# A ConvNeXt block and a Mamba block on one core: batch groups of the convolution, weights on another queue, one transfer for each scan tile

## The chip, the cores and the metric

The kernel runs on one core of a Trainium2 chip. The metric is the device time of one execution in microseconds; the number given for a kernel is the median of its runs. PE is TensorE, DVE VectorE, ACT ScalarE, POOL GpSimd and SP SyncE, which issues nearly all DMAs here. All data is float32.

## The reference, cut to what matters

The input is 32 images of 96 channels and 56 x 56 points (3136 tokens).

```
# layer 0
h = depthwise_conv7x7(x) + conv_b
h = layernorm over channels(h)
x1 = (gelu(h @ w1 + b1) @ w2 + b2) * layer_scale + x
# layer 1: two Mamba layers on seq = x1 as (batch, 3136 tokens, 96)
xs, z = split(layernorm(seq) @ in_w)               # 192 channels each
xc = silu(causal conv of 4 taps over tokens(xs) + conv_b)
dt, Bm, Cm = split(xc @ xproj_w)                   # 6, 16 states, 16 states
delta = softplus(dt @ dt_w + dt_b)
dA  = exp(delta * A);   dBx = delta * Bm * xc      # per channel and state
h_t = dA_t * h_(t-1) + dBx_t                       # 192 x 16 recurrences
y = (sum over states(h * Cm) + Dp * xc) * silu(z)
seq = seq + y @ out_w
# then: 1x1 convolution over (seq, pooled x1), batch norm over everything, + x1
```

## The kernel before

**Tiles of the scan.** An image is cut into 4 chunks of 784 tokens (`CH`), each of two halves of 392 (`HC`). The 192 x 16 recurrences of a chunk are 24 scans of 128 partitions: 6 blocks `j` of 32 channels and 4 groups `g` of 4 states. A partition of a scan tile is one channel of the block with one of the group's four states; before the change the order is (state, channel), that is partition 32 s + m. One chunk in one Mamba layer is a *stage*; there are 256, numbered from 0, and each has 24 *steps*, one scan each.

**A step** (`scan`, `exps`, `spread`, `pooled`, `add_up`). ACT makes `exp(delta * A)` from the tile `d4` of the block (L871). The tile dBx comes in two ways. For blocks 2 and 5 (`POOLED`), POOL multiplies `us` (u = delta * xc, read back with copies for the four states) by the states' B (L897). For the others, PE spreads `u` into PSUM with the 0/1 matrix `sel` (L886, tile `w`) and DVE multiplies it by B (L913). DVE scans (L920) into a ring of four tiles `h`, POOL multiplies by C (L924), and PE sums the four states with `ssum` into `y` (L957). B and C are in `bc` tiles, one per group, with B in the first half of the row and C in the second. `bc`, `d4` and `us` are read from DRAM copies (`bd`, `dd`, `uu`) of small on-chip results, since a DMA can repeat a row for several partitions: `load_bc`, `load_d4` and `load_u` each issue four DMAs per tile, one for each state of the group.

**The order by hand.** The loop is emitted in a fixed order: every other piece of work has a slot, counted in steps of the stage, and `run` emits it there. `prep` prepares the next stage, `post` finishes the last one, `block0` does half a chunk of layer 0 for the following images (its `norm`, tile `hz`, L429, is on DVE at slot 14.1), and `conv` does one channel pair of the 7 x 7 convolution for one group of images. Each of `block0` and `conv` has its slots in one stage at a time, from stage 2 on.

**The convolution.** Two channels x 56 rows fill 112 partitions; the seven vertical taps are in a banded 112 x 112 matrix per horizontal tap. The first group of images goes ahead of the loop (`conv_pair`, 48 pairs, three rotating buffers): DVE fills the bands (L165), SP stores them to `band_d`, PE does 7 matmuls for each half of the images (L176), ACT evicts (`ct`, L180), SP stores. The other groups go through the loop, `NB` images each, two parts of 7 taps (L541), at slots 7.7 to 10.4 and 18.5 to 22.2, with the bands read back. With `NB = 7` there are 11 images ahead and 3 groups x 48 pairs = 144 stages with a convolution (2 to 145).

```
    NB = 7
    b0 = B - 3 * NB if B > 3 * NB else B
...
            at = (7.7, 8.2, 8.6, 9.2, 9.6, 10.2, 10.4), (18.5, 18.6, 19.2, 20.2, 21.2, 21.3, 22.2)
...
            if 2 <= m < len(convs) + 2:
                put(m, conv(*convs[m - 2]))
```

**Ahead of the loop.** After three pairs of the convolution come the weights (about 60 DMAs on SP, in `column`, `blocks`, `norm_weights` and beside them), then the other 45 pairs. There the order is the compiler's priorities, not written by hand, and each queue works in order. Then `block0` makes the first image's eight halves, with ACT alternating between Ln and Exp (the inverse root), Gelu and plain functions; functions of different sets make ACT load a table (`ACT_TABLE_LOAD`). Last, `prep` of stage 0 runs without anything beside it.

**After the loop** the batch norm is applied in a pass over all images.

Of the kernel before, what the change touches and what calls it, by code (L numbers as in the profile page):

```python
# [34 lines left out]
F32 = mybir.dt.float32  # L35
I32 = mybir.dt.int32
AF = mybir.ActivationFunctionType
ALU = mybir.AluOpType
# [6 lines left out]
C = 96  # L45
# [16 lines left out]
def convnext_mamba_kernel(  # L62
# [142 lines left out]
    for a in range(2):  # L205
        r = slice(64 * a, 64 * a + 64)
        for jj in range(2):
            nc.vector.tensor_copy(
                sel[r, jj, :].rearrange("p (s m) -> p s m", s=4),
                ident[r, 64 * a + 32 * jj : 64 * a + 32 * jj + 32]  # L210
                .unsqueeze(1)
                .broadcast_to([64, 4, 32]),
            )
# [3 lines left out]
    nc.vector.tensor_tensor(ssum, ssum, ident[:, 64:96], ALU.add)  # L217
    nc.vector.tensor_tensor(ssum, ssum, ident[:, 96:128], ALU.add)

    def column(src, n, name):  # L220
        t = const.tile([n, 1], F32, name=name, tag=name)
        nc.sync.dma_start(t, src)
        return t

    def blocks(src, name):

        n = src.shape[1]
        t = const.tile([128, NQ, n], F32, name=name, tag=name)
        for a in range(2):
            nc.sync.dma_start(t[64 * a : 64 * a + 64], src.rearrange("(q m) n -> m q n", m=64))  # L230
        return t

    g0, be0 = column(ln0_g, C, "g0"), column(ln0_b, C, "be0")
# [5 lines left out]
    nc.sync.dma_start(ls, lscale.rearrange("c one -> one c").partition_broadcast(128))  # L239
    for f in range(NF):  # L240
        nc.sync.dma_start(b1_sb[:, f : f + 1], b1[f * 128 : (f + 1) * 128, :])
        nc.sync.dma_start(w2_sb[:, f, :], w2[f * 128 : (f + 1) * 128, :])
        nc.vector.tensor_tensor(w2_sb[:, f, :], w2_sb[:, f, :], ls, ALU.mult)
    gpw_sb = const.tile([C, C], F32, name="gpw_sb")
    nc.sync.dma_start(gpw_sb, gp_wt)
    gpb = column(gp_b, C, "gpb")
    fw1 = const.tile([C, C], F32, name="fw1")
    nc.sync.dma_start(fw1, fus_wt[0:C, :])
    fw2 = const.tile([C, C], F32, name="fw2")
    nc.sync.dma_start(fw2, fus_wt[C : 2 * C, :])  # L250
    fusb = column(fus_b, C, "fusb")
    bng, bnb = column(bn_g, C, "bng"), column(bn_b, C, "bnb")

# [3 lines left out]
    def norm_weights(dst, src, g, b):  # L257


        n = src.shape[1]  # L260
        raw = su.tile([C, n], F32, name="raw", tag="raw")
        nc.sync.dma_start(raw, src)
        m = su.tile([C, C + 1], F32, name="m", tag="nm")
        nc.vector.tensor_scalar(m[:, 0:C], center_m, g, None, ALU.mult)
        nc.vector.tensor_copy(m[:, C : C + 1], b)
        ps = sups.tile([128, 512], F32, name="ps", tag="nps")
        nc.tensor.matmul(ps[0 : C + 1, 0:n], m, raw, start=True, stop=True)
        nc.vector.tensor_copy(dst, ps[0 : C + 1, 0:n])

    norm_weights(w1_sb, w1, g0, be0)  # L270
    for i in range(2):
        d = {}
        lg, lb = column(ln_g[i], C, f"lg{i}"), column(ln_b[i], C, f"lb{i}")
        wz = const.tile([C + 1, 2 * DIN], F32, name=f"inw{i}", tag=f"inw{i}")
        norm_weights(wz, in_w[i], lg, lb)
        wx = const.tile([C + 1, 4, DIN], F32, name=f"wx{i}", tag=f"wx{i}")
        nc.sync.dma_start(wx, taps[i].partition_broadcast(C + 1))
# [24 lines left out]
        nc.sync.dma_start(dtw, dt_w[i])  # L302
# [34 lines left out]
    with ExitStack() as main:  # L337
# [55 lines left out]
        def block0(b, c, s):  # L393
# [45 lines left out]
            def gelu():  # L439
                v["gl"] = work([128, NF, HC], "gl", 1)  # L440
                for f in range(NF):
                    nc.scalar.activation(
                        v["gl"][:, f], v["pss"][f][:, 0:HC], AF.Gelu, bias=b1_sb[:, f : f + 1]
                    )
                exp_ln_tables()

            def down():
                v["ps"] = psum(2)
# [48 lines left out]
        with tc.tile_pool(name="p0", bufs=1) as p0, tc.tile_pool(  # L497
            name="pp0", bufs=1, space=PSUM
        ) as pp0:
            pre += [p0, pp0]  # L500
            pieces = [
                (slot + 3 * (2 * c + s), piece)
                for c in range(NCH)
                for s in range(2)
                for slot, *_, piece in block0(0, c, s)
            ]
            for _, piece in sorted(pieces, key=lambda p: p[0]):
                piece()
            pre.clear()

        wp = main.enter_context(tc.tile_pool(name="wp", bufs=2))
# [64 lines left out]
        def prep(S):  # L576
# [142 lines left out]
            def load_u(k):  # L719
                def piece():  # L720
                    t = wp.tile([128, CH], F32, name="us", tag="us", bufs=1)
                    for s in range(4):
                        nc.sync.dma_start(t[32 * s : 32 * s + 32], v["uu"][k])
                    S.us[POOLED[k]] = t

                return piece

            def load_d4(j):
                def piece():
                    t = wp.tile([128, CH], F32, name="d4", tag="d4", bufs=3)  # L730
                    for s in range(4):
# [388 lines left out]
```

## Time and profile before

| | us |
|---|---|
| median of 3 runs (lowest, highest) | 17344.25 (17338.93, 17366.62) |
| the profiled execution, its own time | 17343.56 |
| its span in the profile | 17341.9 |
| last eviction of the first convolution | starts at 433.07 |
| first scan | 574.21 |
| start of stage 2 | 717.04 |
| last scan | 16978.6 |
| final pass | 16998 to 17342 |

The span is the profiled execution from its first to its last instruction. A group's row gives line, engine, operation, tiles and shapes, then the count after `x`, the busy time, the mean of one in ns, and the engine's idle time just before with what ended most of it. A row of the waits says which instruction's engine stood still for which, in total, how often and how long at most. A row of the timeline is start, duration, engine, line and operation, with the idle time before it in brackets; rows of several instructions give the whole stretch. PEclk is the share of PE's clock that was granted.

### The profile page before, as it was taken

The page shows a single profiled execution, that of the slowest core. Times are in us where ns is not written, and L with a number is a line of the kernel's source. Part 1 is how long each engine was busy: PE and PEld are TensorE (multiplying, and loading weights), DVE is VectorE, ACT ScalarE, POOL GpSimd, SP SyncE. Part 2 cuts the span into 40 slices and gives each one's busy share as a digit, 9 for nine tenths or more (in the row PEclk, how much of TensorE's full clock was granted, in tenths as well). Part 3 has the DMA queues.
Part 4 walks back from the last instruction along what each step waited for, and adds up shares of the span by engine and source line. Part 5 has one row for each costly group of instructions (what it writes and reads, how often), then busy time and mean ns, then how long its engine had stood idle before and what let it go on. Part 6 is the DMA issues. An engine that isn't in the chain of part 4 may idle for free. (4 is left out here: it accounts for less than half of the span.)

```text
span 17341.9 us, 217468 instructions
## 1 busy us (share of the span) xinstructions
PE 15452.2 (89%) x67992; PEld 5467.0 (32%) x67992; DVE 16061.7 (93%) x12345; ACT 11459.0 (66%) x18648; POOL 15637.1 (90%) x8737
## 2 busy tenths in 40 slices
PE   8899999999999999999999988888888888888870
PEld 5233333333333333333333322222222222222220
DVE  8699999999999999999999999999999999999994
ACT  1666666666676776666666666666666666666653
POOL 0699999999999999999999999999999999999991
PEclk9899999999999999999999999999999999999985
DMA  4455555555555555555555555555555555555548
GB/s 107 105 138 140 139 136 139 139 140 140 133 141 140 140 140 135 138 140 140 137 136 141 137 129 125 124 131 127 124 126 128 128 125 124 131 128 125 127 113 280
DMA packets 1421981, 2346.44 MB, mean 135 GB/s; under 512 B 629958, under 2 KB 793586, under 8 KB 1420820
## 3 DMA queue, kind: packets, MB, share of 16 engines
q1 hardware_dynamic: 1413652, 2294.00, 53.5%
q10 hardware_dynamic: 7168, 38.54, 0.6%
q8 instruction: 536, 8.78, 0.2%
q14 instruction: 625, 5.12, 0.1%
HBM read 1929.11 MB, written 402.41 MB: 134 GB/s over the span
## 5 line engine op out<-in xcount | busy, mean ns | idle before, releaser
L924 POOL TENSOR_TENSOR da<-h,bc 128x784 f32<-128x784 f32 x6144 | 11295.2, 1861 | 799.0 <-DVE h L920 686.1
L920 DVE TENSOR_TENSOR_SCAN h<-da,st,w 128x784 f32<-128x784 f32 x3072 | 5664.2, 1844 | 324.0 <-ACT st L931 9.4
L957 PE MATMUL y<-da,ssum 128*32 128x392 f32 x24576 | 5131.2, 540 | 429.9 <-POOL da L924 427.5
L913 DVE TENSOR_TENSOR w<-w,bc 128x784 f32<-128x784 f32 x4096 | 3995.7, 976 | 284.0 <-PE w L886 114.6
L897 POOL TENSOR_TENSOR da<-us,bc 128x784 f32<-128x784 f32 x2048 | 3816.3, 1863 | 2.9 <-DMA us<-uu 2.9
L871 ACT ACTIVATE da<-d,A 128x784 f32<-128x784 f32 x4096 | 3757.6, 941 | 43.6 <-DMA d<-dd 27.7
L871 ACT ACTIVATE w<-d,A 128x784 f32<-128x784 f32 x2048 | 1878.8, 918 | 2662.8 <-DVE h L920 2270.2
L920 DVE TENSOR_TENSOR_SCAN h<-w,st,da 128x784 f32<-128x784 f32 x1536 | 2712.4, 1827 | 5.9 <-ACT w L871 4.8
L622 PE MATMUL ps<-hn,wx 97*64 97x392 f32 x12288 | 2262.6, 503 | 7.9 <-DVE hn L610 7.9
L957 PEld LDWEIGHTS y<-da,ssum 128*32 128x32 f32 x24576 | 1093.7, 115 | 3700.0 <-issue 2095.1
L920 DVE TENSOR_TENSOR_SCAN h<-da,w 128x784 f32<-128x784 f32 x1024 | 1827.0, 1784 | 107.9 <-ACT st L931 3.8
L886 PE MATMUL w<-u,sel 64*128 64x392 f32 x4096 | 1028.4, 581 | 638.5 <-DVE h L920 637.4
L622 PEld LDWEIGHTS ps<-hn,wx 97*64 97x64 f32 x12288 | 795.3, 136 | 1429.1 <-issue 1111.3
L701 POOL TENSOR_TENSOR u<-dl,xc 128x784 f32<-128x784 f32 (+1 forms) x512 | 736.8, 1439 | 543.0 <-ACT dl L687 543.0
L951 PE MATMUL y<-xc,D 128*128 128x392 f32 x1536 | 796.6, 604 | 252.1 <-DVE z L938 246.1
L541 PE MATMUL ps<-xpad,band 112*112 112x224 f32 (+1 forms) x4032 | 1003.0, 358 | 0.0
L361 ACT ACT_TABLE_LOAD x759 | 973.8, 1283 | 14.5 <-PEq L1107 0.8
L370 ACT ACTIVATE sq<-ps 96x392 f32<-96x392 f32 x768 | 340.7, 490 | 812.6 <-PE ps L365 464.3
L920 DVE TENSOR_TENSOR_SCAN h<-w,da 128x784 f32<-128x784 f32 x512 | 872.3, 1766 | 0.0
L541 PEld LDWEIGHTS ps<-xpad,band 112*112 112x112 f32 x4032 | 583.8, 175 | 832.5 <-issue 783.5
L679 PE MATMUL ps<-dbl,dtw 6*64 6x392 f32 x3072 | 688.3, 511 | 99.9 <-ACT dbl L657 99.9
L886 PEld LDWEIGHTS w<-u,sel 64*128 64x128 f32 x4096 | 327.7, 196 | 1229.6 <-DVE h L920 1055.3
(124 smaller groups left out, 14412.7 us busy)
## 6 DMA issues: line engine op xcount, KB each, us to landing
bc<-bd SPq DMA_DIRECT2D x4096, 196.0 KB, 5.3
d<-dd SPq DMA_DIRECT2D x6144, 98.0 KB, 2.8
us<-uu SPq DMA_DIRECT2D x2048, 98.0 KB, 2.2
dd<-dl SPq DMA_DIRECT2D x512, 294.0 KB, 3.8
uu<-u SPq DMA_DIRECT2D x1024, 49.0 KB, 1.6
band<-band_d SPq DMA_DIRECT2D x144, 343.0 KB, 3.5
cv<-conv_d SPq DMA_DIRECT2D x256, 147.0 KB, 2.4
xin<-in_x SPq DMA_DIRECT2D x128, 294.0 KB, 3.8
```

The source lines that it names most:

```text
L361: nc.scalar.preload_act_table_set("natural_log_exp_and_others")
L541: nc.tensor.matmul(v["ps"][0:R2, 0 : (last - first) * W], v["band"][:, dw, :], xpad[:, first:last, dw : dw + W], start=(dw == 0), stop=(dw ...
L622: nc.tensor.matmul(v["x", q][rows(a), 0:HC], weights[:, k, 64 * q : 64 * q + 64], v["hn"][:, o : o + HC], start=(k == 0), stop=(k == last),)
L701: nc.gpsimd.tensor_tensor(S.u[:, lo:hi], v["dl"][:, lo:hi], S.xc[:, lo:hi], ALU.mult)
L871: nc.scalar.activation(e, S.d4[j], AF.Exp, scale=S.d["A"][:, j, g : g + 1])
L886: nc.tensor.matmul(S.u4[:, 512 * a : 512 * a + HC], sel[rows(a), j % 2, :], S.u[rows(a), j // 2, :], start=True, stop=True,)
L897: nc.gpsimd.tensor_tensor(t, S.us[j], S.bcs[g][:, 0, :], ALU.mult)
L913: nc.vector.tensor_tensor(halves(db), S.u4.rearrange("p (a b) -> p a b", a=2)[:, :, 0:HC], halves(S.bcs[g][:, 0, :]), ALU.mult,)
L920: nc.vector.tensor_tensor_scan(ring[:, g, :], S.e.pop((j, g)), db, 0.0 if c == 0 else d["st"][:, j, g : g + 1], ALU.mult, ALU.add,)
L924: nc.gpsimd.tensor_tensor(da, ring[:, g, :], S.bcs[g][:, 1, :], ALU.mult)
L951: nc.tensor.matmul(S.y[:, 0:HC], S.d["D"][:, q, :], S.xc[:, q, :], start=True, stop=False)
L957: nc.tensor.matmul(S.y[r0 : r0 + 32, 0:HC], ssum, da[:, tok(a)], start=False, stop=(g == NG - 1),)
```

## The change

1. `NB` becomes 5: 12 images ahead of the loop, 4 groups of 5 in it, so 192 stages (2 to 193) with a convolution of 3 + 2 images instead of 4 + 3.
2. A scan tile's partitions are ordered (channel, state), 4 m + s. So `load_d4` and `load_u` can bring a tile with one DMA that repeats each row four times, and `load_bc` a half of a `bc` tile with one DMA that repeats four rows 32 times: 16 instead of 48 DMAs in a stage. `sel`, `ssum` and `A` follow the new order; `A` is now gathered with a mask `own` instead of by partition blocks.
3. All weights ahead of the loop, but those of the first convolution, are issued from POOL: 61 DMAs in the place of 57 on SP.
4. In the first image, the two halves of a chunk have the same slots, instead of following one another, and the requests for the Ln and Exp table are placed before the pair's root.

```diff
-    NB = 7
-    b0 = B - 3 * NB if B > 3 * NB else B
+    NB = 5
+    b0 = B - 4 * NB if B > 4 * NB else B
...
-                sel[r, jj, :].rearrange("p (s m) -> p s m", s=4),
+                sel[r, jj, :].rearrange("p (m s) -> p m s", s=4),
...
-    nc.vector.tensor_tensor(ssum, ident[:, 0:32], ident[:, 32:64], ALU.add)
...
+    nc.vector.tensor_reduce(ssum, ident.rearrange("p (m s) -> p m s", s=4), AX.X, ALU.add)
+    own = su.tile([128, 4], F32, name="own", bufs=1)
+    nc.vector.tensor_reduce(own, ident.rearrange("p (m s) -> p s m", s=4), AX.X, ALU.add)
+    nc.vector.tensor_scalar(own, own, -1.0, None, ALU.mult)
...
-        nc.sync.dma_start(t, src)
+        nc.gpsimd.dma_start(t, src)
...
-        for s in range(4):
-            r = slice(32 * s, 32 * s + 32)
-            nc.sync.dma_start(ar[r], a_log[i].rearrange("(q m) n -> m q n", m=32))
-            nc.scalar.activation(A[r], ar[r, :, s::4], AF.Exp)
-        nc.vector.tensor_scalar(A, A, -1.0, None, ALU.mult)
+        for j in range(2 * NQ):
+            src = a_log[i][32 * j : 32 * j + 32, :]
+            nc.gpsimd.dma_start(ar[:, j, :], src.unsqueeze(1).broadcast_to([32, 4, NS]))
+        nc.scalar.activation(ar, ar, AF.Exp)
+        nc.vector.tensor_scalar(A, ar[:, :, 0::4], own[:, 0:1], None, ALU.mult)
+        for s in range(1, 4):
+            nc.vector.scalar_tensor_tensor(
+                A, ar[:, :, s::4], own[:, s : s + 1], A, ALU.mult, ALU.add
+            )
...
             def root():
+                if pre and s == 0:
+                    exp_ln_tables()
                 rsqrt(v["ps"])
...
-                exp_ln_tables()
+                if not pre:
+                    exp_ln_tables()
...
-                (slot + 3 * (2 * c + s), piece)
+                (slot + 4 * c, piece)
...
+            exp_ln_tables()
             pre.clear()
...
-                        for s in range(4):
+                        for k in range(2):
+                            src = v["bd"][NS * k + 4 * g : NS * k + 4 * g + 4, :]
                             nc.sync.dma_start(
-                                t[32 * s : 32 * s + 32],
-                                v["bd"][4 * g + s :: NS, :].partition_broadcast(32),
+                                t[:, k, :], src.unsqueeze(0).broadcast_to([32, 4, CH])
                             )
...
-                    for s in range(4):
-                        nc.sync.dma_start(t[32 * s : 32 * s + 32], v["uu"][k])
+                    nc.sync.dma_start(t, v["uu"][k].unsqueeze(1).broadcast_to([32, 4, CH]))
...
-                        nc.sync.dma_start(
-                            t[32 * s : 32 * s + 32], v["dd"][32 * j : 32 * j + 32, :]
-                        )
+                    src = v["dd"][32 * j : 32 * j + 32, :]
+                    nc.sync.dma_start(t, src.unsqueeze(1).broadcast_to([32, 4, CH]))
```

More of the change, by code (lines that the diff above doesn't have):

```diff
@@ L208, in convnext_mamba_kernel @@
             nc.vector.tensor_copy(
-                sel[r, jj, :].rearrange("p (s m) -> p s m", s=4),
+                sel[r, jj, :].rearrange("p (m s) -> p m s", s=4),
                 ident[r, 64 * a + 32 * jj : 64 * a + 32 * jj + 32]
-                .unsqueeze(1)
-                .broadcast_to([64, 4, 32]),
+                .unsqueeze(2)
+                .broadcast_to([64, 32, 4]),
             )
     ssum = const.tile([128, 32], F32, name="ssum")
-    nc.vector.tensor_tensor(ssum, ident[:, 0:32], ident[:, 32:64], ALU.add)
-    nc.vector.tensor_tensor(ssum, ssum, ident[:, 64:96], ALU.add)
-    nc.vector.tensor_tensor(ssum, ssum, ident[:, 96:128], ALU.add)
+    nc.vector.tensor_reduce(ssum, ident.rearrange("p (m s) -> p m s", s=4), AX.X, ALU.add)
+    own = su.tile([128, 4], F32, name="own", bufs=1)
+    nc.vector.tensor_reduce(own, ident.rearrange("p (m s) -> p s m", s=4), AX.X, ALU.add)
+    nc.vector.tensor_scalar(own, own, -1.0, None, ALU.mult)
     def column(src, n, name):
         t = const.tile([n, 1], F32, name=name, tag=name)
-        nc.sync.dma_start(t, src)
+        nc.gpsimd.dma_start(t, src)
         return t
@@ L229, in blocks @@
         for a in range(2):
-            nc.sync.dma_start(t[64 * a : 64 * a + 64], src.rearrange("(q m) n -> m q n", m=64))
+            nc.gpsimd.dma_start(t[64 * a : 64 * a + 64], src.rearrange("(q m) n -> m q n", m=64))
         return t
@@ L238, in convnext_mamba_kernel @@
     ls = su.tile([128, C], F32, name="ls", bufs=1)
-    nc.sync.dma_start(ls, lscale.rearrange("c one -> one c").partition_broadcast(128))
+    nc.gpsimd.dma_start(ls, lscale.rearrange("c one -> one c").partition_broadcast(128))
     for f in range(NF):
-        nc.sync.dma_start(b1_sb[:, f : f + 1], b1[f * 128 : (f + 1) * 128, :])
-        nc.sync.dma_start(w2_sb[:, f, :], w2[f * 128 : (f + 1) * 128, :])
+        nc.gpsimd.dma_start(b1_sb[:, f : f + 1], b1[f * 128 : (f + 1) * 128, :])
+        nc.gpsimd.dma_start(w2_sb[:, f, :], w2[f * 128 : (f + 1) * 128, :])
         nc.vector.tensor_tensor(w2_sb[:, f, :], w2_sb[:, f, :], ls, ALU.mult)
     gpw_sb = const.tile([C, C], F32, name="gpw_sb")
-    nc.sync.dma_start(gpw_sb, gp_wt)
+    nc.gpsimd.dma_start(gpw_sb, gp_wt)
     gpb = column(gp_b, C, "gpb")
     fw1 = const.tile([C, C], F32, name="fw1")
-    nc.sync.dma_start(fw1, fus_wt[0:C, :])
+    nc.gpsimd.dma_start(fw1, fus_wt[0:C, :])
     fw2 = const.tile([C, C], F32, name="fw2")
-    nc.sync.dma_start(fw2, fus_wt[C : 2 * C, :])
+    nc.gpsimd.dma_start(fw2, fus_wt[C : 2 * C, :])
     fusb = column(fus_b, C, "fusb")
@@ L261, in norm_weights @@
         raw = su.tile([C, n], F32, name="raw", tag="raw")
-        nc.sync.dma_start(raw, src)
+        nc.gpsimd.dma_start(raw, src)
         m = su.tile([C, C + 1], F32, name="m", tag="nm")
@@ L276, in convnext_mamba_kernel @@
         wx = const.tile([C + 1, 4, DIN], F32, name=f"wx{i}", tag=f"wx{i}")
-        nc.sync.dma_start(wx, taps[i].partition_broadcast(C + 1))
+        nc.gpsimd.dma_start(wx, taps[i].partition_broadcast(C + 1))
         for k in range(4):
@@ L301, in convnext_mamba_kernel @@
         dtw = const.tile([DTR, DIN], F32, name=f"dtw{i}", tag=f"dtw{i}")
-        nc.sync.dma_start(dtw, dt_w[i])
+        nc.gpsimd.dma_start(dtw, dt_w[i])
         d["dtw"] = dtw
@@ L730, in piece @@
                     t = wp.tile([128, CH], F32, name="d4", tag="d4", bufs=3)
-                    for s in range(4):
-                        nc.sync.dma_start(
-                            t[32 * s : 32 * s + 32], v["dd"][32 * j : 32 * j + 32, :]
-                        )
+                    src = v["dd"][32 * j : 32 * j + 32, :]
+                    nc.sync.dma_start(t, src.unsqueeze(1).broadcast_to([32, 4, CH]))
                     S.d4.append(t)
```

## The prediction

> **What bounds the kernel now.** I read the page's busy rows, then the timeline for the length of a stage, then VectorE's waits, then the windows for the clock.
>
> ```profile
> span 17341.9 us, 217468 instructions
> PE 15452.2 (89%) x67992; PEld 5467.0 (32%) x67992; DVE 16061.7 (93%) x12345; ACT 11459.0 (66%) x18648; POOL 15637.1 (90%) x8737
> ...
> L924 POOL TENSOR_TENSOR da<-h,bc 128x784 f32<-128x784 f32 x6144 | 11295.2, 1861 | 799.0 <-DVE h L920 686.1
> L920 DVE TENSOR_TENSOR_SCAN h<-da,st,w 128x784 f32<-128x784 f32 x3072 | 5664.2, 1844 | 324.0 <-ACT st L931 9.4
> ...
> L913 DVE TENSOR_TENSOR w<-w,bc 128x784 f32<-128x784 f32 x4096 | 3995.7, 976 | 284.0 <-PE w L886 114.6
> ```
>
> Per stage DVE has 24 scans and 16 products (24 x 1.82 + 16 x 0.976 = 59.3 us), five 0.55 us operations and a sixth in 248 stages; POOL has 32 products of 1.86 us and 2.9 us more. Both fill a stage of about 64 us. No step of the change touches these instructions, so the loop can lose only its stalls. First scans of stages 2, 146 and 250:
>
> ```profile
> 717.04 1.79 DVE L920 TENSOR_TENSOR_SCAN h<-da,w 128x784 f32<-128x784 f32 x1 [3.81 <-ACT st L931]
> ...
> 9912.09 1.79 DVE L920 TENSOR_TENSOR_SCAN h<-da,w 128x784 f32<-128x784 f32 x1
> ...
> 16585.00 1.79 DVE L920 TENSOR_TENSOR_SCAN h<-da,w 128x784 f32<-128x784 f32 x1
> ```
>
> The 144 stages that carry a convolution take 9195.05/144 = 63.86 us, the 104 without one 6672.91/104 = 64.16. Less work, yet longer. The waits of DVE, up to 9850 us and after it, say why:
>
> ```profile
> DVE w L913 <- PE w L886: 94.5, 157, 2.3
> ...
> DVE hz L429 <- ACT ps L382: 95.1, 76, 2.3
> ```
>
> With convolution DVE waits for PE's spread (`w`) at the stage's end; without it, for `hz`, whose chain starts with two PE matmuls. Four windows (columns: PE, PEld, DVE, ACT, POOL, PEclk, DMA share, GB/s), two of a stage with convolution, two without:
>
> ```profile
> 1888.00:1895.00 7.00, 6.76 (x32) 2.73 (x28) 6.87 (x5) 3.94 (x7) 7.00 (x5) 1.00 0.35 98
> 1907.00:1914.00 7.00, 7.00 (x18) 2.23 (x16) 6.73 (x7) 4.70 (x8) 5.89 (x4) 0.58 0.68 149
> 11085.00:11092.00 7.00, 2.59 (x14) 0.66 (x12) 7.00 (x5) 4.50 (x8) 7.00 (x5) 0.86 0.46 125
> 11092.00:11099.00 7.00, 7.00 (x14) 2.52 (x14) 6.73 (x6) 3.23 (x8) 6.53 (x5) 0.50 1.05 226
> ```
>
> At steps 8 to 10 (four short scans on pooled tiles) only the taps keep PE busy. Without them it works 2.59 of 7 us, the clock halves, and `hz` is late. With them it stays at 1.00 there; in about one stage in five it halves later (0.58), at step 14, and the stalls fall at steps 19 and 23.
>
> **The change, part by part.** The sum is made against the profiled execution, 17343.6 us (span 17341.9); the median of the runs is 17344.25, so both stand alike.
>
> *First convolution, 12 batches.* PE sets its pace: successive `ct` evictions are 4.00 us apart for a 336-column half and 3.33 for a 280-column one (53.42, 57.42, 60.75 us). Two 336 halves make 8.0 instead of 7.33 us: 48 x 0.67 = +32. DVE's seven 1.04 us copies per pair (7.3) then lie beneath PE.
>
> *Weights through GpSimd's queue.*
>
> ```profile
> 43.89 24.14 PE L176 MATMUL ps<-xpad,band 112*112 112x336 f32 x84 [43.89 <-DMA xpad<-in_x]
> ...
> 97.53 0.32 SPq L160 DMA_DIRECT2D xpad<-in_x  x1
> ...
> 100.90 19.31 PE L176 MATMUL ps<-xpad,band 112*112 112x336 f32 x63 [2.43 <-DMA xpad<-in_x]
> ```
>
> The fourth pair's input stands in SP's queue behind the weights until 97.5; PE's hole from 68.0 to 100.9 is 33 us. In the changed order SP issues `xpad` loads at once, and POOL 61 DMAs from about 9 us. Behind them wait: DVE, in order, with the scale of `D` and `A` of layer 1 (55th and 61st) ahead of the last band copies of pair 4; ACT with its two `ar` exponentials among the first five evictions; SP, whose stores of those evictions stand ahead of later `xpad` loads. No DMA from POOL is in the trace. Nearest row: SP issued nearly the same weights from 42.1 to 97.5, 0.9 us each; the upper price is below. I take 1.2: the last lands at 9 + 61 x 1.2 + 2 = 84, pair 4's band is ready at 88, PE needs it at 43.9 + 4 x 8 + 6 = 82. Stall 6; weight matmuls left on PE about 5. The last `ct` moves from 433.6 to 43.9 + 384 + 5 + 6 + 0.5 = 439: **+6**, with bounds 0 and +35 (2 us a DMA).
>
> A rule speaks against this. Row: DVE's band copies run back to back at 1.04 us. The Trainium skill, "SBUF — State Buffer", section "SBUF: two separate sides", warns that a DMA from GpSimd needs its descriptors written by that engine, locked out while DVE runs a two-port operation; its example grows from 0.62 to 3.1 us. By that price (13 DMAs gone before the copies start at 25, 48 x 3.1) the last lands at 176, the stall is 98 instead of 6, and the whole sum 17336 instead of 17244. But 784 elements in 1.04 us is far from a doubled rate, so I stay by the row and keep the price for the range.
>
> *First batch's halves in pairs.* ACT, 436 to 522 us:
>
> ```profile
> L442 ACT ACT_TABLE_LOAD x13 | 16.7, 1283 | 0.2
> ...
> L381 ACT ACT_TABLE_LOAD x6 | 7.7, 1283 | 0.1
> L382 ACT ACT_TABLE_LOAD x6 | 7.7, 1283 | 0.1
> ```
>
> 25 loads; in the changed order Gelu, Ln and Exp of two halves stand together: 4 + 3 + 3 = 10. The explicit preload in `root` isn't placed there, so Ln and Exp still load apart. 15 x 1.283 = 19 us off ACT, which sets this stretch, and 3 us of its 23 us of waits: **-22** (bounds -12, -30).
>
> *Single transfers, (channels, states).* SP issues 16 instead of 48 DMAs a stage for `bc`, `d4`, `us`; bytes and row lengths stay, `sel`, `ssum` and `A` only permute. In the loop DVE waits for no DMA and POOL 47 us in total, behind DVE's pace: 0. Where a stage's preparation isn't ahead (stages 0, 1 and the last), the burst is awaited:
>
> ```profile
> 565.00:570.00 5.00, 5.00 (x18) 1.70 (x16) 0.00 (x0) 0.00 (x0) 0.00 (x0) 0.50 1.05 230
> ...
> 17000.00:17342.00 342.00, 0.00 (x0) 0.00 (x0) 114.44 (x64) 108.30 (x64) 0.00 (x0) 0.50 1.01 338
> ```
>
> 4.5 MB take 20 us at about 230 GB/s with all engines busy; full-width transfers of the last pass reach 338. Bounds per burst 0 and -6; I take -4, three times: **-12**.
>
> *Convolution over 192 stages.* 48 more stages keep their taps. A tap pass streams 168 and 112 columns instead of 224 and 168. A 392-column pass takes 0.33 us at full clock, so 56 columns are 0.047 us; 14 passes per half: 0.65 us off PE ahead of the spreads at steps 11 and 23. Mean excess over a free step in a convolution stage: 0.13 at step 11, 0.13 at 19, 0.40 at 23, in all 0.66; without convolution 1.0 at step 13. Step 11's goes, the other two lose part: I take 0.30 off a convolution stage (bounds 0 and 0.66). So 144 x 0.30 = -43, and 48 x (0.30 + 0.30) = -29: **-72** (-16 to -143). ACT's 96 more evictions (0.42 us) lie in its 19 us of idle a stage; 48 more `band` loads lie under a DMA share of 0.57.
>
> Does the clock hold with shorter taps? I summed the matmul streaming in each 3.41 us window between the trace's clock records: half clock follows where it filled under about 0.38, never above 0.40 (apart from the windows of the six-row dt matmuls). With the taps shortened in place, convolution stages still have 0.32 such windows each, nearly all at step 14. The skill, "TensorE: Matmul & The Clock Gate", section "What's actually happening", halves the clock after an idle window; the trace's limit is stricter than idle. By the rule alone a stage without convolution (2.59 of 7 us busy) would keep its clock, its stall of 1.0 us would have another cause, and neither the 48 stages nor the fourth rival would count: 17344 - 28 - 43 = 17273. By the trace the taps hold the clock, with little to spare: 17244.
>
> Sum: 6 - 22 - 12 - 72 = -100: 17343.6 - 100 = **17244 us**.
>
> **The rivals.**
> - *The loop's stalls stay as they are.* They come from the half-clock window at step 14, which the taps don't cause. Then only 48 x 0.30 = -15 remains: 17344 - 28 - 15 = 17300. Against it: late spreads directly follow taps. 0.17.
> - *All stalls go:* -143 - 28 gives 17173. 0.12.
> - *GpSimd's DMAs are slow* (2.5 to 3.1 us): +60 to +90 on the forecast, 17305 to 17335, no measurable change. 0.08.
> - *Slower: the shorter taps let the clock fall at steps 8 to 10 as well.* Then 192 stages have the stall at step 13 on top of the others: 64.16 + 0.66 = 64.82. 144 x 0.96 + 48 x 0.66 = +170, less 28: 17486. It decides from +0.33 us a stage (63 us over 192 stages, against the 28 gained at the start). For it: 0.38 against 0.40 is a thin margin. Against: seven taps still spread over the steps. 0.08.
> - That single transfers don't spread over the DMA engines would show as a DMA share near 1 in the loop; 32 channels times 4 copies leave no reason. Within the remainder.
>
> **How the numbers follow.** The forecast has 0.55, its own range is 17190 to 17305. The range 17165 to 17345 takes in the first four cases. 0.2% is 35 us, about what a measurement of this kernel tells from no change: faster means below 17309.6. Faster: nearly all of the forecast, the first two rivals, 0.79; same 0.11 (slow DMAs, a half-missed loop); slower 0.10.
>
> **What would show it.** PE without a hole near 70 to 100 us and the last `ct` near 439; the first scan near 554 us (574.2 + 6 - 22 - 4); 10 table loads in the first batch; stages with convolution near 63.5 us up to stage 193 and 64.2 after it; `w L913 <- PE w L886` well under 94 us, `hz` at less than half of 95. Wrong if POOL's last weight lands after 110 us, if convolution stages exceed 63.9, or if `hz` waits grow.

## The result, and the profile after

| | before | after |
|---|---|---|
| median of the comparison's runs (lowest, highest), us | 17356.46 (17338.93, 17373.69) | 17276.21 (17259.54, 17286.65) |
| ratio, 95% interval | | 0.9951, 0.9940 to 0.9962 |
| profiled execution, its own time, us | 17343.56 | 17286.65 |

Faster by about 80 us of medians. The forecast was 17244, which is 100 below the profiled execution it was summed against, with 17165 to 17345 as the range. The profiled execution of the changed kernel is the slowest of its five runs, so the two traces differ by 57 us of span (17341.9 to 17284.9), and the stages below are accounted against these 57.

The page's busy rows and the three groups that fill the loop:

```profile
span 17284.9 us, 207580 instructions
...
PE 15488.9 (90%) x69336; PEld 5550.7 (32%) x69336; DVE 16068.6 (93%) x12351; ACT 11452.6 (66%) x18723; POOL 15673.1 (91%) x8798
...
L932 POOL TENSOR_TENSOR da<-h,bc 128x784 f32<-128x784 f32 x6144 | 11302.5, 1863 | 749.6 <-DVE h L928 656.6
L928 DVE TENSOR_TENSOR_SCAN h<-da,st,w 128x784 f32<-128x784 f32 x3072 | 5666.0, 1844 | 319.9 <-ACT st L939 4.6
...
L921 DVE TENSOR_TENSOR w<-w,bc 128x784 f32<-128x784 f32 x4096 | 3997.2, 976 | 229.5 <-PE w L894 58.5
```

One scan and one product cost DVE the same as before (1844 and 976 ns), and POOL 1863 for 1861 ns. What fell is idle time: the one ahead of the products `w` went from 284.0 to 229.5 us. So the time came from the start and from stalls, as argued. First scans of stages 0, 2, 146, 194 and 250 in the timeline:

```profile
559.39 1.79 DVE L928 TENSOR_TENSOR_SCAN h<-da,w 128x784 f32<-128x784 f32 x1
...
697.73 1.79 DVE L928 TENSOR_TENSOR_SCAN h<-da,w 128x784 f32<-128x784 f32 x1
...
9872.63 1.79 DVE L928 TENSOR_TENSOR_SCAN h<-da,w 128x784 f32<-128x784 f32 x1
...
12928.00 1.79 DVE L928 TENSOR_TENSOR_SCAN h<-da,w 128x784 f32<-128x784 f32 x1
...
16525.19 1.79 DVE L928 TENSOR_TENSOR_SCAN h<-da,w 128x784 f32<-128x784 f32 x1
```

Stage 2 now starts at 697.73 (717.04 before): 19 us from the start. Stages 2 to 249 take 16525.19 - 697.73 = 15827.5 (15868.0 before): 40 us from the loop. The rest, stage 250 to the end, took 3 us more. DVE's waits from 700 to 12910 us, which spans the stages 2 to 193, and then from 12960 to 16500:

```profile
DVE hz L438 <- ACT ps L389: 45.1, 30, 2.1
DVE w L921 <- PE w L894: 30.3, 44, 1.1
DVE z L946 <- PE y L965: 24.5, 21, 1.5
```

```profile
DVE hz L438 <- ACT ps L389: 54.7, 39, 2.3
```

The kernel before has 94.5 us of `w` from 700 to 12910 as well, and for `hz`:

```profile
DVE hz L429 <- ACT ps L382: 42.5, 33, 2.3
```

All of this `hz` comes from the stages 146 to 193, which had no convolution then. Now they have one, yet `hz` is as large as it was. It sits in convolution stages: taken between successive scans as a mean over stages 10 to 145, the excess over the shortest step went from 0.04 to 0.29 us at step 13, while it fell from 0.18 to 0.05 at step 11 and from 0.45 to 0.19 at step 23. Two windows of the changed kernel, 27.8 us into stages 20 and 21 (columns: PE, PEld, DVE, ACT, POOL, PEclk, DMA share, GB/s), show why:

```profile
1872.00:1878.80 6.80, 6.43 (x12) 2.70 (x12) 6.53 (x7) 3.47 (x9) 6.30 (x4) 0.50 0.94 310
1937.20:1944.00 6.80, 6.12 (x23) 2.31 (x24) 6.53 (x7) 3.81 (x8) 6.29 (x4) 1.00 0.88 339
```

In stage 20 the clock is at half from 27.8 to 34.6 us, which is from the end of step 10 to the start of step 13, and PE gets 12 matmuls through where stage 21 gets 23; `hz` is then 1.4 us late. A half-clock window reaches into steps 10 or 11 in 25 of the stages 10 to 145, in none before. Of all 192 convolution stages 35 have one. They take 64.90 us on average and the other 157 take 63.43; step 13 is long only in stages of the first kind.

The start, in the timeline. GpSimd's queue, then PE, then ACT's evictions around the gap and the last one:

```profile
13.60 0.53 POOL L244 DMA_DIRECT2D b_sb<-in_b  x1
23.70 0.53 POOL L245 DMA_DIRECT2D w_sb<-in_w  x1 [9.57 <-DMA g<-in_ln_g]
...
37.35 0.51 POOL L225 DMA_DIRECT2D lg<-in_ln_g  x1 [8.02 <-DMA gpw_sb<-in_gp_wt]
45.09 0.51 POOL L225 DMA_DIRECT2D lb<-in_ln_b  x1 [7.23 <-DMA gpb<-in_gp_b]
...
67.71 3.31 POOL L316 DMA_DIRECT2D ar<-in_a_log  x6
```

```profile
46.69 1.57 PE L270 MATMUL ps<-raw,m 96*97 96x384 f32 x2 [46.69 <-DMA raw<-in_w]
48.05 26.41 PE L176 MATMUL ps<-xpad,band 112*112 112x336 f32 x84
...
79.82 4.79 PE L176 MATMUL ps<-xpad,band 112*112 112x336 f32 x10
...
88.17 42.18 PE L176 MATMUL ps<-xpad,band 112*112 112x336 f32 x147
```

```profile
86.06 0.54 ACT L180 ACTIVATE ct<-ps,cb 112x336 f32<-112x336 f32 x1 [11.03 <-PE ps L176]
...
442.68 0.54 ACT L180 ACTIVATE ct<-ps,cb 112x336 f32<-112x336 f32 x1 [3.40 <-PE ps L176]
```

A DMA costs POOL 0.5 to 0.7 us. What POOL loses is in standing still for landings, 25 us in three places, with eight of its DMAs under way each time. PE's 33 us hole is gone; a gap of 11 us between evictions is left, and the convolution begins at 48.05 in place of 43.89. The last `ct` starts at 442.68 (433.07 before), with one image more.

ACT's table loads in the first image, 446 to 508 us, 10 where there were 25:

```profile
L451 ACT ACT_TABLE_LOAD x4 | 5.1, 1283 | 0.1
L388 ACT ACT_TABLE_LOAD x3 | 3.8, 1283 | 0.1
L389 ACT ACT_TABLE_LOAD x3 | 3.8, 1283 | 0.1
```

And the transfers: the page's queue row before and after (packets, MB, share of the 16 engines), and the issues after.

```profile
q1 hardware_dynamic: 1413652, 2294.00, 53.5%
...
q1 hardware_dynamic: 1292712, 2308.46, 42.1%
...
bc<-bd SPq DMA_DIRECT2D x2048, 392.0 KB, 6.3
d<-dd SPq DMA_DIRECT2D x1536, 392.0 KB, 3.9
us<-uu SPq DMA_DIRECT2D x512, 392.0 KB, 3.4
```

A transfer of half a `bc` tile lands later than one of a quarter did (6.3 for 5.3 us), but the engines are busy for a fifth less.

### The profile page after: what moved, and what is told of

It is laid out like the page before. It is cut to its first block, busy times and chain, and to the rows that moved or that the text cites. A ratio compares the mean times of both kernels' runs of the same rounds, so it can differ in the third digit from the quotient of the medians.

```text
span 17284.9 us, 207580 instructions
## 1 busy us (share of the span) xinstructions
PE 15488.9 (90%) x69336; PEld 5550.7 (32%) x69336; DVE 16068.6 (93%) x12351; ACT 11452.6 (66%) x18723; POOL 15673.1 (91%) x8798
## 3 DMA queue, kind: packets, MB, share of 16 engines
q1 hardware_dynamic: 1292712, 2308.46, 42.1%
## 5 line engine op out<-in xcount | busy, mean ns | idle before, releaser
L932 POOL TENSOR_TENSOR da<-h,bc 128x784 f32<-128x784 f32 x6144 | 11302.5, 1863 | 749.6 <-DVE h L928 656.6
L928 DVE TENSOR_TENSOR_SCAN h<-da,st,w 128x784 f32<-128x784 f32 x3072 | 5666.0, 1844 | 319.9 <-ACT st L939 4.6
L921 DVE TENSOR_TENSOR w<-w,bc 128x784 f32<-128x784 f32 x4096 | 3997.2, 976 | 229.5 <-PE w L894 58.5
L879 ACT ACTIVATE da<-d,A 128x784 f32<-128x784 f32 x4096 | 3763.7, 941 | 31.4 <-DMA d<-dd 15.4
L552 PE MATMUL ps<-xpad,band 112*112 112x168 f32 (+1 forms) x5376 | 1087.1, 312 | 0.0
L552 PEld LDWEIGHTS ps<-xpad,band 112*112 112x112 f32 x5376 | 710.3, 175 | 1088.3 <-issue 1025.7
L368 ACT ACT_TABLE_LOAD x759 | 973.8, 1283 | 14.1 <-PEq L1115 0.8
```

Of the source, the lines that this page charges most:

```text
L552: nc.tensor.matmul(v["ps"][0:R2, 0 : (last - first) * W], v["band"][:, dw, :], xpad[:, first:last, dw : dw + W], start=(dw == 0), stop=(dw ...
L879: nc.scalar.activation(e, S.d4[j], AF.Exp, scale=S.d["A"][:, j, g : g + 1])
L921: nc.vector.tensor_tensor(halves(db), S.u4.rearrange("p (a b) -> p a b", a=2)[:, :, 0:HC], halves(S.bcs[g][:, 0, :]), ALU.mult,)
L928: nc.vector.tensor_tensor_scan(ring[:, g, :], S.e.pop((j, g)), db, 0.0 if c == 0 else d["st"][:, j, g : g + 1], ALU.mult, ALU.add,)
L932: nc.gpsimd.tensor_tensor(da, ring[:, g, :], S.bcs[g][:, 1, :], ALU.mult)
```

## The experiments

For each run, from its trace: start of the last `ct`; the first image, from the first load of `cv` to the last `fb`; start of stage 2; mean stage, from the first scans of stages 2 and 194, and of 194 and 250; then the median, and the ratio to the kernel before in its own comparison. Times in us.

| kernel | last ct | first image | stage 2 | 2 to 193 | 194 to 249 | median | ratio (95%) |
|---|---|---|---|---|---|---|---|
| before | 433.1 | 85.2 | 717.0 | 63.93 | 64.18 | | 1 |
| after | 442.7 | 61.7 | 697.7 | 63.70 | 64.24 | 17276.2 | 0.9951 (0.9940 to 0.9962) |
| e1_weights_sp | 466.5 | 63.4 | 723.3 | 63.58 | 64.28 | 17295.0 | 0.9962 (0.9947 to 0.9977) |
| e2_nb7 | 413.0 | 61.8 | 666.3 | 64.04 | 64.19 | 17313.1 | 0.9969 (0.9957 to 0.9980) |
| e3_halves_serial | 442.8 | 82.9 | 717.2 | 63.67 | 64.18 | 17291.5 | 0.9959 (0.9944 to 0.9974) |
| e4_quarters | 444.0 | 63.2 | 702.5 | 63.63 | 64.24 | 17283.5 | 0.9954 (0.9937 to 0.9971) |
| e5_long_taps | 443.5 | 61.5 | 698.7 | 63.53 | 64.14 | 17238.5 | 0.9937 (0.9922 to 0.9952) |
| e6_warm_rest | 443.1 | 62.2 | 698.7 | 63.61 | 63.35 | 17214.0 | 0.9925 (0.9908 to 0.9941) |
| e7_warm_all | 443.8 | 62.9 | 700.2 | 63.56 | 63.26 | 17198.8 | 0.9914 (0.9899 to 0.9929) |
| e8_single_old_order | 432.4 | 84.7 | 774.8 | 81.28 | 79.95 | 21724.5 | 1.2522 (1.2504 to 1.2541) |
| e9_order_alone | 436.6 | 88.3 | 716.5 | 64.04 | 64.18 | 17362.3 | 1.0001 (0.9992 to 1.0010) |
| e10_conv_alone | 462.1 | 85.1 | 745.9 | 63.72 | 64.24 | 17331.1 | 0.9983 (0.9976 to 0.9990) |

The runs were taken in four comparisons, in which the kernel before had medians of 17356.5 (after), 17362.7 (e1 to e4), 17346.1 (e5 to e8) and 17360.6 us (e9, e10). So medians of different comparisons are not subtracted from each other; where a time is set against the changed kernel below, it is by the ratios.

How far a profiled execution can be trusted: after, e1, e3, e4 and e6 have the same convolution stages (e4 with other transfers), and their means for 2 to 193 lie between 63.58 and 63.70, with the changed kernel's own profile at the top. That is 24 us over 192 stages. A part of it is how many stages have the half-clock window: 35 in the changed kernel, 25 in e1, at about 1.5 us each. The rest has no cause that I know, so a loop's mean is read to about 0.1 us; the starts are read to a few us.

**The four parts, each undone in the changed kernel.** The intervals of these four overlap that of the changed kernel, so the time alone does not part them; the stage of the trace that each part should touch does.

*The weights, back on SP* (`nc.gpsimd.dma_start` to `nc.sync.dma_start` in the weights' helpers):

```diff
-        nc.gpsimd.dma_start(t, src)
+        nc.sync.dma_start(t, src)
```

> The changed kernel with all weights issued from SP's queue again. Theory (the fourth pair's input stands behind the weights in SP's queue): PE has its hole of about 33 us again after the third pair, less the 11 us of waits that the changed kernel has left there, so the last ct eviction moves from 442.7 to about 465 us and the time grows by 20 to 25 us, to about 17300. Rival (GpSimd's DMAs cost as much as they free): last ct within 5 us of 442.7, no change. The rest of the kernel, loop and table loads, as in the changed kernel.

The last `ct` starts 23.8 us later, at 466.5, and stage 2 25.6 us later; by the ratios the time is 19 us higher. The timeline of PE has the hole again:

```profile
69.81 1.45 PE L270 MATMUL ps<-raw,m 96*97 96x384 f32 x4
95.21 1.57 PE L270 MATMUL ps<-raw,m 96*97 96x384 f32 x2 [23.95 <-DMA raw<-in_in_w]
...
104.89 25.36 PE L176 MATMUL ps<-xpad,band 112*112 112x336 f32 x81 [3.87 <-DMA xpad<-in_x]
```

So the queue is worth about 24 us at the place where it acts. (The loop of this profiled execution was 24 us shorter, within what was said of means, and its span is no longer than that of the changed kernel.)

*Seven images a batch again*:

```diff
-    NB = 5
-    b0 = B - 4 * NB if B > 4 * NB else B
+    NB = 7
+    b0 = B - 3 * NB if B > 3 * NB else B
```

> The changed kernel with NB = 7: 11 images ahead, 144 stages with a convolution. Theory (stages with a convolution are the shorter ones, and shorter taps make them shorter still): the first convolution ends 32 us earlier (last ct near 411), but the stages 2 to 145 go back to about 63.86 us (+20 us) and the stages 146 to 193 to about 64.15 (+24 us); net +12 us, near 17288. Rival (the spread over 192 stages isn't what shortens the loop, the single transfers are): stages keep 63.7 us up to 145, and the kernel is 10 to 30 us faster than the changed one.

The start loses one image, stage 2 comes 31.4 us earlier, as expected. The loop pays more than was expected: 64.04 for 63.70 us over 192 stages is 65 us where 44 were expected, and by the ratios the time is 31 us higher. DVE's waits from 700 to 12910 are those of the kernel before, `w` foremost:

```profile
DVE w L921 <- PE w L894: 105.0, 154, 2.2
DVE hz L438 <- ACT ps L389: 46.5, 35, 2.3
```

So the fall of `w` belongs to the batches of five, not to the new order.

*The first image's halves serial, with the old table requests*:

```diff
-                (slot + 4 * c, piece)
+                (slot + 3 * (2 * c + s), piece)
```

> The changed kernel with the first image's halves one after the other and the table requests where they were. Theory (25 instead of 10 table loads on ACT): the stretch from the first cv load to the image's bias grows from 61.7 to about 85 us, and the time by about 23 us, to about 17300. Rival (PE at half clock sets this stretch): it grows by less than 10 us.

The first image takes 82.9 us for 61.7, with 25 loads for 10; that is 21.2 us longer, and 14 us by the ratios. The last `ct` and the loop stay where they were.

*Four DMAs a tile again, in the new order* (the same in `load_bc` and `load_u`):

```diff
-                    nc.sync.dma_start(t, src.unsqueeze(1).broadcast_to([32, 4, CH]))
+                    for s in range(4):
+                        nc.sync.dma_start(t[s::4], v["dd"][32 * j : 32 * j + 32, :])
```

> The changed kernel, partitions still (channel, state), but bc, d4 and us with four DMAs each again, every one to each fourth partition. Theory (single transfers only shorten the bursts that are awaited): the loop stays at 63.7 us a stage up to 193; first scan +1, stages 0 and 1 +4, the last stages +4: about +10 us, near 17286, and a DMA share of 53% again. Rival (the lighter load on the DMA engines, 42 instead of 53%, is what shortened the loop): stages with a convolution go up by 0.1 us or more, +30 us in all.

Stage 2 comes 4.8 us later, of which 1.3 is already in the last `ct`; by the ratios the time is 5 us higher, which the intervals don't tell from nothing. The loop's stages are not longer (63.63), so the rival of this run falls. The queue's share is 46.7%, between the 53.5 of the kernel before and 42.1; 53 had been expected.

**What the order and the convolution do alone.** The kernel with only part 2 of the change:

> Of the change only the tile order (channels, states) with single transfers; seven images a batch with convolution over 144 stages, serial halves and the weights on SP's queue are as in the kernel before. Theory: the order's worth is the shorter bursts at the ends, 9 to 10 us by the changed kernel's profile (first scan, first stages, last stages), and nothing in the loop, whose transfers were hidden: the stages 2 to 193 stay at about 63.93 us, w <- PE w stays at 0.6 to 0.7 us a stage, the time is about 17347. Rival: the order brings the loop's gain, because the transfers need a fifth less time of the DMA engines (42 for 53 per cent of them): then the stages fall to 63.7 us and the time to about 17305.

No difference: 1.0001. The ends gain as in the changed kernel or more (`fb` to the first scan -1.3, from there to stage 2 -5.7, stage 250 to the last scan -8.2). But the last `ct` comes 3.5 us later and the first image takes 3.1 longer, the loop's stages are 0.11 us longer (64.04 for 63.93, 21 us in all), and the wait for PE's spread is larger:

```profile
DVE w L917 <- PE w L890: 110.8, 156, 2.2
```

It was 94.5 in the kernel before and is 105.0 in e2, which has this order and these batches too. Two traces agree, but 0.11 is hardly more than the scatter above; why the order should lengthen this wait is open. The rival, that a lower share of the DMA engines brings the loop's gain, falls here too: the share is 41.3%, and the loop gained nothing.

The kernel before with batches of five and nothing else:

> Of the change only the convolution over 192 stages (batches of five images, twelve before the loop); the rest is as in the kernel before. Theory: the loop's gain is all of this edit: the stages 2 to 193 go from 63.93 to 63.7 us (-40), w <- PE w falls from 0.65 to 0.2 us a stage and hz <- ACT ps appears at about 0.2; but the twelve images before the loop cost 30 to 34 us, the last ct starts at about 465: the time is about 17350, no change that is sure. Rival: the loop's gain needs the new tile order too: the stages stay at 63.9 us and the time is about 17387.

The loop gains 0.21 us a stage, 40 us over 192, nearly all of the 44 that the changed kernel gained there, with the old order and 53.7% of the DMA engines; `w` and `hz` move as in the changed kernel:

```profile
DVE hz L429 <- ACT ps L382: 42.9, 28, 1.9
DVE w L913 <- PE w L886: 36.4, 42, 4.0
```

The start pays 28.9 us (stage 2 at 745.9). The median is 29 us below, more than the 11 that these two leave, and than the 6 of its profiled span; the mechanism is as expected, the size isn't settled between 17 and 42 us (the interval). The convolution spread over 192 stages is a good trade only because the other parts shorten the start.

**Does the clock cost the rest of the loop's gain?** The first part of the loop's convolution gets a fourth image:

```diff
+                last = max(last, first + 4) if part == 0 else last
```

> The changed kernel with the convolution's first part in the loop taking four images (224 columns) in place of three (168), as its second part does; one image is computed twice with the same result. Theory: in the changed kernel TensorE's granted clock halves at steps 10 and 11 of some convolution stages, because the shorter taps leave it less busy there, and this makes the wait of hz for ScalarE's ps (45 us between 700 and 12910 us, 30 times). With taps a third longer that wait falls to 15 us or less, the stages up to 193 go from a mean of 63.70 to about 63.5 us, and the time falls by 25 to 40 us, to about 17240. Rival: the halving has nothing to do with the taps' length; then hz stays near 45 us, VectorE's w waits for TensorE's w again as in the kernel before (0.6 us a stage) because TensorE has more to do, and the time is 17276 to 17350.

The mechanism is as expected: `hz` is gone from the top of the waits from 700 to 12910 (0.8 us are left), and part of `w` comes back:

```profile
DVE w L922 <- PE w L895: 57.9, 77, 1.8
DVE z L947 <- PE y L966: 15.1, 13, 1.5
DVE h L929 <- DVE w L922: 3.9, 8, 0.5
```

In the window of stage 20 that was shown above, the clock is whole:

```profile
1866.90:1873.70 6.80, 6.30 (x23) 2.44 (x24) 6.53 (x7) 3.92 (x10) 6.34 (x4) 1.00 0.88 341
```

Of the 192 convolution stages none has a half-clock window at steps 10 or 11 now. The stages 2 to 193 are 0.17 us shorter (32 us in all). By the ratios the kernel, which does more work, is 24 us faster than the changed one; the two intervals overlap, so it is the stages that show the gain.

**The stages without a convolution.** Seven matmuls whose result nobody reads go where a convolution stage has its first taps:

```diff
+                    nc.tensor.matmul(
+                        v["ps"][0:R2, 0 : 4 * W], warm_w, xpad[:, 0:4, dw : dw + W],
+                        start=(dw == 0), stop=(dw == 6),
+                    )
...
+            at = (7.7, 8.2, 8.6, 9.2, 9.6, 10.2, 10.4)
...
+            elif m >= 2:
+                put(m, warm())
```

> The changed kernel plus seven matmuls of 224 columns, whose result nothing reads, put into the stages from 194 on (which have no convolution) where a convolution stage has its taps. Theory: those stages take 64.24 us on average against 63.70 with a convolution because TensorE's clock falls to half between the taps' places and the eviction ps behind it comes late for hz (0.98 us a stage); idle taps keep the clock up, the stages 194 to 249 take 63.4 to 63.6 us, and the time falls by 35 to 45 us, to about 17235. Rival: the difference is not TensorE's clock but what else a convolution stage changes; then the extra matmuls only delay w or y, the stages stay at 64.2 us or grow, and the time is 17276 to 17310.

The stages 194 to 249 fall from 64.24 to 63.35 us, the shortest of all: 50 us over 56 stages. In the changed kernel 51 of these 56 have a half-clock window at steps 10 or 11, and no other stage of them has the long step 13; here none has one. The waits from 12960 to 16500 no longer have `hz` at all:

```profile
DVE z L966 <- PE y L985: 7.2, 6, 1.5
DVE w L941 <- PE w L914: 3.0, 7, 1.8
```

Two windows 27 us into stages 210 and 211, of the changed kernel and then of this one:

```profile
13985.10:13992.10 7.00, 6.52 (x20) 2.47 (x20) 6.73 (x7) 4.15 (x10) 7.00 (x5) 0.76 0.88 338
14047.20:14054.20 7.00, 5.87 (x11) 2.60 (x12) 6.86 (x6) 3.58 (x8) 6.74 (x5) 0.51 0.92 331
```

```profile
13950.00:13957.00 7.00, 7.00 (x28) 2.98 (x27) 6.73 (x7) 4.12 (x10) 6.88 (x4) 1.00 0.98 372
14012.00:14019.00 7.00, 7.00 (x30) 2.72 (x28) 6.81 (x6) 4.93 (x12) 6.70 (x5) 1.00 0.86 327
```

PE has more to do and its clock is whole, so the evictions for `hz` come in time: work without any use took the stall away. By the ratios the kernel is 45 us faster, about the 50 us of these stages. (Its profile has 17 us less in the stages 2 to 193 as well, where nothing was changed: 63.61 for 63.70, within what was said of means.)

Both edits together:

> The two edits of the other kernels of this call together: four images in the first convolution part of the loop and idle taps in the stages without a convolution. Theory: the gains add, as they lie in different stages: 60 to 85 us below the changed kernel, about 17200. Rival: the first edit brings the wait of w back, which eats its gain, and only the second's is left: about 17235.

The result is 17198.81 us, by the ratios 64 us below the changed kernel; the parts give 32 + 50 = 82 by their stages and 24 + 45 = 69 by their ratios. In the convolution stages 2.4 us of `hz` are left, and `w` is at 58.3 as in e5. It has the lowest median of all versions, and its interval (0.9899 to 0.9929) lies clear of that of the changed kernel, though not of e6's.

**What the order is needed for.** The kernel before with single transfers, in its own order (states, channels), so that the outermost dimension of the source is a four (the copies in `us` and `d4`, the states in `bc`):

```diff
-                    for s in range(4):
-                        nc.sync.dma_start(t[32 * s : 32 * s + 32], v["uu"][k])
+                    nc.sync.dma_start(t, v["uu"][k].unsqueeze(0).broadcast_to([4, 32, CH]))
```

> The kernel before with the tiles' old order (states, channels) but single transfers, the four copies being the outermost dimension of the source. Theory: what the new order is for is that a transfer is shared out over the DMA engines by its outermost dimension; with four there, four engines carry everything. The changed kernel's transfers take 42 per cent of 16 engines' time, so four would need 168 per cent, some 107 us a stage: the loop is bound by transfers, about 27000 us, and VectorE's and GpSimd's work waits for da, d4 or bc. Rival: the sharing does not look at the outermost dimension; then it is the changed order's gain of fewer and larger transfers with the kernel before's convolution: the loop as before, some 10 us gained in the first scan's start and at the end, 17340 to 17350.

A quarter slower. Waits from 960 to 16600 us, all engines:

```profile
ACT sq L370 <- DMA conv_d<-sq: 2855.0, 142, 28.2
...
DVE hz L429 <- ACT ps L382: 2437.4, 144, 25.4
```

The tile `sq` has three buffers, which the convolution's outputs share with layer 0's squares. A square waits up to 28 us until the convolution's store from the same buffer has landed, and `hz` waits behind it. The store is short, but SP issues it between the scan's tiles:

```profile
8061.88 7.15 SPq L668 DMA_DIRECT2D bc<-bd  x4
...
8073.31 4.26 SPq L557 DMA_DIRECT2D conv_d<-sq  x1
...
8089.83 0.49 ACT L370 ACTIVATE sq<-ps 96x392 f32<-96x392 f32 x1 [20.24 <-DMA conv_d<-sq]
```

The page's queue row has only 32.1% of the engines' time: transfers can bound a kernel far below a share of 1. From the trace's packet records between 8000 and 9000 us, the share of time with so many packets under way:

| packets under way | 0 | 1 to 3 | 4 or 5 | 6 to 13 | 14 and more |
|---|---|---|---|---|---|
| after | 0.46 | 0.07 | 0.02 | 0.10 | 0.35 |
| e8 | 0.05 | 0.04 | 0.74 | 0.07 | 0.09 |

Most of the time four packets are under way here (0.62 of it), and the commonest number above that in the changed kernel is sixteen, as if four and sixteen engines carried the tiles; the trace's records don't name the engine. This agrees with the Trainium skill's "DMA: Bandwidth & Descriptors", section "Rules for kernel authors": an outermost dimension of a size c below 16 confines a transfer to c engines at most. The packets' summed time is the same in both: 6835 us in these 1000 us of the changed kernel, or 435 us in a stage of 63.7, and 5332 in e8, or 435 us in a stage of 81.6. The expected 107 us a stage put all of it on four engines; but only the repeated tiles go there, 16 x 392 of about 8500 KB a stage. If packet time goes with the bytes, that is 435 x 0.74 / 4 = 80 us, an estimate; 80 to 81 were measured. So the theory holds, and its number was for more bytes than the tiles have.

## Why the prediction was right, and where it was off

The total was right by its wide range more than by its terms: the medians differ by 80 us, and the two profiles by 57 of the 100 forecast. Each of the four parts shows in its own stage of the trace; the largest term was nearly twice too big. By the prediction's own steps, profile against profile:

| step | predicted | measured |
|---|---|---|
| first convolution and weights | +6 | +9.6 (last `ct`) |
| first image | -22 | -23.5 (85.2 to 61.7) |
| single transfers at the ends | -12 | -9.6 (-1.1, -4.5 and -4.0) |
| convolution over 192 stages | -72 | -40.5 (stages 2 to 249) |
| after the last scan | 0 | +6.9 (363.3 to 370.2) |

*The step that was mis-sized* is "I take 0.30 off a convolution stage", and under it "convolution stages still have 0.32 such windows each, nearly all at step 14". Of the stalls in a convolution stage, step 11's went and step 23's fell by 0.26, as forecast or better; step 19's stayed (0.18 to 0.20). What was not in the sum is the 0.25 that came at step 13. That count was made on the old trace with the taps shortened where they stood; in the run, 25 of 136 stages have a half-clock window at steps 10 or 11. Matmul streaming, summed in the trace as the prediction did it (0.33 us for 392 columns), shows that PE lacks work there: in those 35 of the 192 stages it fills 0.36 of the 3.41 us ahead of the fall at the median and 0.43 at most. In the other stages no window near that place is filled less than 0.44, and with the longer taps (e5) none less than 0.42. The fourth rival, with the chance of 0.08, named this mechanism and its place; it priced it for all stages, 0.96, where about a quarter of that came. With it taken away (e5) the stages are at 63.53, and 192 x (63.93 - 63.53) = 76 is about the 72 that I had summed. So the reason was right, and the clock's price was left out of the likeliest case. The 40.5 itself is read from one profile of each kernel: the other kernels with the same convolution stages (e1, e3, e4, e6) would give 50 to 68 over the 192 stages, where this profile gives 44. (The bounds of that term, -16 and -143, come to -15 and -141 by the prediction's own figures.)

*POOL's DMAs* were costed at 1.2 us, with 3.1 as the rule's price. They take 0.5 to 0.7, also between 64.6 and 70.8 us, while DVE's band copies run back to back at 1.04, and the transfers land meanwhile: the lock that the Trainium skill's "SBUF — State Buffer", section "SBUF: two separate sides", warns of does not show with these copies there. The last weight is issued near 71 instead of landing at 84. The place of my price was taken by another thing, the 25 us of waiting for landings, and by a start of the convolution that is 4 us later. In the first of these waits DVE does nothing. In the other two, from 29 to 45 us, its band copies run as well, so the lock is not ruled out there; but in the kernel before, with no DMA on POOL, SP's input loads of the same time, issued from 23.5 us on, let PE begin only at 43.89. That the two errors cancelled to within 4 us is luck.

*The first image* came as summed. e3 confirms it by itself.

*Single transfers* came as summed at the ends, but e9 shows that as an edit alone they are worth nothing, with a start and a loop that are rather slower. What the order does is to allow single transfers at all: in the old order they would cost a quarter of the time (e8). I had set that rival aside because "32 channels times 4 copies leave no reason", which holds for the changed order only; the chances of the forecast and of the four rivals ahead of it sum to 1, so it had none left.

*The rule on the clock.* By the rule alone (the clock falls after an idle window) the stages without convolution would have another cause of their stall and 17273 would have been the forecast, which is closer to 17276 than 17244. It is closer by chance: in e6 the stall goes when the clock stays whole, and the clock falls after windows in which PE is working (2.59 of 7 us in the prediction's third window), not idle.

*After the last scan.* 363 us in the one profile of the kernel before, 365 to 377 in the other kernels' profiles (368 in e9, 366 in e10). No part of the change is tied to it.

## What to carry to other kernels

A stage with less work can be the longer one: compare stages by what they carry, and look at the granted clock in the few microseconds ahead of the stall, not at its mean (0.93 to 0.94 in both kernels here). Where the clock falls in such a place, matmuls without use, put in the right slots, can pay (50 us in 56 stages here). When work is spread thinner to clear one stall, ask whether what is left still holds the clock. And a transfer that repeats rows should have a long dimension outermost (32 in all the transfers of the changed kernel, channels or copies) and the four inside. When it is the other way round, the share of DMA time in the profile does not show it; the number of packets under way does.

## What the runs showed of the hardware that I had not expected

- A DMA issue costs GpSimd 0.5 to 0.7 us. Three times GpSimd stood still with eight of its DMAs under way (7.2 to 9.6 us), until the oldest had landed; the first eight, issued from 8.8 to 14.1 us, landed at 23.4 to 25.3. Why they took so long is open; SP's transfers of the same time are the likely cause.
- The same bytes in the same row lengths cost the DMA engines less time in the order (channels, states): 53.5% with four DMAs in the old order, 46.7% with four in the new (e4), 42.1% with one. Packets of 2 to 3 KB took 209 ns at the median before and 124 in both forms of the new order.
- Seven more matmuls in a stage, at a place where TensorE was running at half clock, made the stage 0.89 us shorter (64.24 to 63.35 us).
- A window of half clock at this one place costs a convolution stage 1.5 us (64.90 for 63.43), and how many stages have one differs between kernels with the same convolution stages (35, 25, 39, 24 and 30 of 192).
